# A graph-network layer on one core: the node update stored in runs of consecutive nodes, the flag for the general pass computed inside the loop, and the last three edge groups as softmax batches of their own

## The chip, the cores and the metric

The kernel runs on one core of one Trainium2 chip. The core has five engines, each with its own queue of instructions that it takes in order: TensorE (PE in the profile, with its weight loads shown apart as PEld), VectorE (DVE), ScalarE (ACT), GpSimd (POOL) and SyncE (SP). [...] Sixteen DMA engines move data between the chip's memory (HBM) and the on-chip memory (SBUF); matrix products land in PSUM. The metric is the device time of one execution in microseconds (us), and the figure that counts is the median of several executions.

## What is computed

One message-passing layer over 12,500 nodes with 64 features and 412,500 edges sorted by receiver, each with 32 features. The reference, cut to what matters:

```python
def layer(node_features, edge_features, senders, receivers, ...):
    act = jax.nn.swish
    msg_in = concatenate([node_features[senders], node_features[receivers], edge_features], -1)
    messages = act(msg_in @ W1 + b1) @ W2 + b2
    att_logits = act(msg_in @ Wa1 + ba1) @ Wa2 + ba2
    att = jax.nn.softmax(att_logits, axis=0)            # over ALL edges
    messages = messages * att
    aggregated = segment_sum(messages, receivers, num_segments=n_nodes)
    upd_in = concatenate([node_features, aggregated], -1)
    return act(upd_in @ Wu1 + bu1) @ Wu2 + bu2

h = maximum(layernorm(x), 0)
x = x + layer(h, edge_attr_32, src, dst, ...)
```

The softmax is over all the edges at once, so nothing can be normalised until the last edge has been seen; and the node update at the end needs the finished sums of all messages.

## The kernel before

**Node phase.** The nodes are padded to NP = 12,544 = 128 x NB with NB = 98; node number = p * 98 + b. The layer norm is computed and two tables of 128 columns go to HBM: `ts_d`, what a sender adds to the hidden layer, and `tr_d`, what a receiver adds.

**Edge loop** (`one_pass`, lines 278 to 555). The edges go through in NG = 403 groups of 1,024 (K = 8 columns of 128). For each group:

- `load(g)` (L351), called two groups ahead: POOL issues 8 indirect DMAs (L358) that gather the senders' rows of `ts_d` into `gs`; SP fetches the edge features, the receivers' numbers and a window of `tr_d`; DVE builds a one-hot matrix (`eo`, L379); PE adds edge and receiver part into `pe` (L385).
- `begin(g)` (L388): DVE adds `pe` to `gs` (L390), which waits for the gathers; ACT takes the tanh (L391).
- `end(g)` (L393): DVE forms the message activations (`acts`, L399), the attention activations (L402), multiplies by the attention vector (L404) and sums to logits `lg` (L407). At the end of a batch, `top` (L411) finds the maximum and PE transposes it (L422, tile `mt`).
- `weigh(s)` (L425): running maximum `nmax`, rescale factor `scale`, exponentials `p` for the batch s.
- `sum_up(g)` (L492), a generator in three steps that lags the loop by about five groups: one-hot of receivers in a window of 40 nodes (L442), weights (L452), 8 matmuls into `sp` (L456), copy (L462), projection to the 64 hidden units of the node update (L467), and `put` (L469), which adds the result into `sums` in SBUF (L477, L480) and notes the maximum in force (L481).

A batch is B = 4 groups. `starts` (L289) makes batches of four, then one of two groups (400 and 401) and one of one group (402). A group can only be summed after its batch has been weighed. After the last groups (L539 to 544) what has not yet been summed is drained: at g = 400 up to group 398, at g = 401 all the rest up to 401, before `begin(402)` comes on DVE's queue, and at g = 402 the last group. `pin` fixes the program order of an instruction within its engine's queue; what is not pinned, a list scheduler places.

During groups 16 and later, `node_bias` (L252) computes each node's own part of the update, four columns b at a time, and stores it to `bu_d`; `node_rest` stores x plus the output bias in `xb_d`.

**Node update** (L558 to 601). When `sums` is complete, 13 chunks of 8 columns b (the last one of 2) are processed, the two halves of a chunk stacked on partitions 0 to 63 and 64 to 127. `sums` holds node p * 98 + b at that very column, while a chunk wants the nodes ordered b first:

```python
sv = sums[:, :NP].rearrange("f (p b) -> f b p", b=NB)     # L563
```

so ACT (L581, `fac`) and DVE (L586, `uT`, once per half) read `sums` with a step of 98 words from element to element. Then DVE adds the bias `bu_in` (L589), ACT takes the tanh (L591), DVE finishes the swish (L592), PE does n matmuls with `uT[:, i, :]` as the weights (L596), DVE adds `xb` (L598), and SP stores the result (L601). Tiles rotate through 3 buffers (`fac` and `th` through 2). Chunk c is written below as L598(c) and so on.

**Flag.** If a receiver falls out of its window, a general pass (`general`) must redo everything. `far` holds three maxima that are known by group 40; after the node update `worst` is formed from them (L604 to 613), combined through `res` tiles so that it follows the last stores, and written to `wrong`. Every engine then loads `wrong` into a register (L246) and branches past `general` (L248).

Of the kernel before, what the change touches and what calls it, by code (L numbers as in the profile page):

```python
# [41 lines left out]
F32 = mybir.dt.float32  # L42
I32 = mybir.dt.int32
AF = mybir.ActivationFunctionType
ALU = mybir.AluOpType
AX = mybir.AxisListType
# [4 lines left out]
P = 128  # L51
D = 64
DE = 32
U = 64
C = 2 * U
# [19 lines left out]
def gnn_kernel(ctx: ExitStack, tc: tile.TileContext, n_edges, x, src, dst, dst_row, first, edge,  # L75
# [14 lines left out]
    hT_d = dram.tile([D, NB, P], F32, name="hT_d")  # L90
    bu_d = dram.tile([U, NB, P], F32, name="bu_d")
    xb_d = dram.tile([NP, D], F32, name="xb_d")

# [157 lines left out]

def node_bias(tc, b, v, work, ps):  # L252

    nc = tc.nc
    NB, w_node = v["NB"], v["w_node"]
    n = min(4, NB - b)
    hb = work.tile([D + 1, 4, P], F32, name="hb")
    nc.vector.memset(hb[D:, :, :], 1.0)
    nc.sync.dma_start(hb[:D, :n, :], v["hT_d"][:, b:b + n, :])
    pb = ps.tile([P, 4, P], F32, name="mt")  # L260
    nc.tensor.matmul(pb[:U, :n, :], w_node[:, 2 * C:], hb[:, :n, :], start=True, stop=True)
    bu = work.tile([U, 4, P], F32, name="bu")
    nc.scalar.copy(bu[:, :n, :], pb[:U, :n, :])
    nc.sync.dma_start(v["bu_d"][:, b:b + n, :], bu[:, :n, :])

# [12 lines left out]
def one_pass(tc, n_edges, v):  # L278
# [4 lines left out]
                       "far", "wrong"))  # L283
    ts_d, tr_d, bu_d, edge, dst_row = (v[k] for k in ("ts_d", "tr_d", "bu_d", "edge", "dst_row"))
    wa2, ba2_c, w2b, wu1a, wu2, we, gather = (
        v[k] for k in ("wa2", "ba2_c", "w2b", "wu1a", "wu2", "we", "gather"))
    ACTS, WINS, AHEAD = 8, 3, 2

    starts = list(range(0, NG - 1, B)) + [NG - 1]  # L289
    NS = len(starts)  # L290
# [4 lines left out]
    with ExitStack() as ctx:  # L295
# [27 lines left out]
        with tc.tile_pool(name="work2", bufs=2) as work2, \  # L323
# [64 lines left out]
            def begin(g):  # L388

                pin(nc.vector.tensor_tensor(gss[g], pes[g], gss[g], ALU.add))  # L390
                pin(nc.scalar.activation(pes[g], gss[g], AF.Tanh))  # L391

            def end(g):  # L393

                s = batch[g]
                if g == starts[s]:
                    lgs[s] = small.tile([P, B * K], F32, name="lg")
                gs, th = gss.pop(g), pes.pop(g)
                pin(nc.vector.scalar_tensor_tensor(acts[g % ACTS][:, :, 0:U], th[:, :, U:C], 1.0,  # L399
                                                   gs[:, :, U:C], op0=ALU.add, op1=ALU.mult))  # L400
                att = work2.tile([P, K, U], F32, name="att")
# [6 lines left out]
                if g == starts[s] + size[s] - 1:  # L408
                    mts[s] = top(s)

            def top(s):  # L411
# [106 lines left out]
            for g in range(NG):  # L518
                more = None
                if done <= g - B - 1 and g < NG - 1 or g == NG - 2 and done < starts[batch[g]]:  # L520
                    more, done = sum_up(done), done + 1
                begin(g)
                if more:
                    next(more)
# [13 lines left out]

                if g >= NG - 3:  # L539
                    upto = starts[batch[g]] - 1 if g == NG - 3 else g + 1  # L540
                    for i in list(range(done, upto)) + [None, None] * (g > NG - 3):
                        for _ in sum_up(i):
                            pass
                    done = max(done, upto)
                if g == min(30, NG):
# [3 lines left out]
                if g == min(40, NG):  # L549
                    pin(nc.vector.tensor_reduce(far[:, 1:2], dloc, AX.X, ALU.min, negate=True))  # L550
                if g >= 16 and g // 4 - 4 < -(-NB // 4):
                    if g % 4 == 2:
                        node_bias(tc, (g // 4 - 4) * 4, v, work2, one_ps)
                    elif g % 4 == 0:
                        node_rest(tc, (g // 4 - 4) * 4, v, work2)


        with tc.tile_pool(name="upd1", bufs=1) as upd1, \  # L558
# [3 lines left out]
            out_v = v["out"].rearrange("(p b) d -> p b d", b=NB)  # L562
            sv = sums[:, :NP].rearrange("f (p b) -> f b p", b=NB)  # L563
            last = nmax[:, NS:NS + 1]
            ones = upd1.tile([P, P], F32, name="ones")
            nc.vector.memset(ones, 1.0)
            all_ps = upd_ps.tile([P, P], F32, name="worst_ps", bufs=1)
            nc.tensor.matmul(all_ps[:, 0:1], ones, total, start=True, stop=True)
            inv = upd1.tile([P, 1], F32, name="inv")
            nc.vector.reciprocal(inv, all_ps[:, 0:1])  # L570

            assert NB % 2 == 0
            for c in range(0, NB, 2 * H):
                n = min(H, (NB - c) // 2)
                bu = work.tile([P, H, P], F32, name="bu_in")
                for h in range(2):
                    nc.sync.dma_start(bu[h * U:(h + 1) * U, :n, :], bu_d[:, c + h * n:c + (h + 1) * n, :])
                xb = work.tile([P, 2 * H, D], F32, name="xb")
                nc.sync.dma_start(xb[:, :2 * n, :], xb_v[:, c:c + 2 * n, :])
                fac = work.tile([U, 2 * H, P], F32, name="fac", bufs=2)  # L580
                nc.scalar.activation(fac[:, :2 * n, :], sv[U:, c:c + 2 * n, :], AF.Exp, bias=last[U:],  # L581
                                     scale=-1.0)
                uT = work.tile([P, H, P], F32, name="uT")
                for h in range(2):
                    cols = slice(h * n, (h + 1) * n)
                    nc.vector.scalar_tensor_tensor(  # L586
                        uT[h * U:(h + 1) * U, :n, :], sv[:U, c + h * n:c + (h + 1) * n, :], inv[:U],
                        fac[:, cols, :], op0=ALU.mult, op1=ALU.mult)
                nc.vector.tensor_tensor(uT[:, :n, :], uT[:, :n, :], bu[:, :n, :], ALU.add)  # L589
                th = work.tile([P, H, P], F32, name="th", bufs=2)  # L590
                nc.scalar.activation(th[:, :n, :], uT[:, :n, :], AF.Tanh, scale=0.5)  # L591
                nc.vector.scalar_tensor_tensor(uT[:, :n, :], th[:, :n, :], 1.0, uT[:, :n, :],  # L592
                                               op0=ALU.add, op1=ALU.mult)
                po = upd_ps.tile([P, H, 2, D], F32, name="po")
                for i in range(n):
                    nc.tensor.matmul(po[:, i, :, :], uT[:, i, :], wu2h, start=True, stop=True)  # L596
                res = work.tile([P, 2 * H, D], F32, name="res")
# [5 lines left out]

            worst = upd1.tile([P, 1], F32, name="worst")  # L604
            nc.vector.tensor_reduce(worst, far, AX.X, ALU.max)
            worst_ps = upd_ps.tile([P, P], F32, name="worst_ps", bufs=1)
            nc.tensor.transpose(worst_ps, worst.to_broadcast([P, P]), ident)
            nc.vector.tensor_reduce(worst, worst_ps, AX.X, ALU.max)
            two = [work.tile([P, 2 * H, D], F32, name="res") for _ in range(3)]
            for t in two:  # L610
                nc.vector.tensor_scalar(t[:, 0, 0:1], worst, 0.0, None, op0=ALU.is_gt)
            nc.vector.tensor_tensor(two[0][:, 0, 0:1], two[0][:, 0, 0:1], two[1][:, 0, 0:1], ALU.max)
            nc.vector.tensor_tensor(wrong, two[0][:, 0, 0:1], two[2][:, 0, 0:1], ALU.max)

# [217 lines left out]
```

## Time and profile before

| | us |
|---|---|
| median of 3 runs (lowest, highest) | 4304.88 (4300.02, 4320.17) |
| the profiled execution, its own time | 4310.41 |
| its span, first to last instruction | 4308.7 |
| POOL busy in the span, almost all of it gather issues | 3166.1 |
| DVE busy | 2544.5 |
| PE busy (modelled ends) | 2221.4 |
| ACT busy | 595.8 |

| stretch of the profiled execution | from, to (us) |
|---|---|
| last gather issue of POOL | 4220.68, 4221.62 |
| `begin(402)` on DVE (L390) | 4229.27 |
| last write to `sums` (L481) ends | 4240.82 |
| last L598 ends | 4297.13 |
| `wrong` written (L613) ends | 4298.58 |
| end of the span | 4308.7 |

A row of a group reads: line, engine, operation, output <- input with their shapes, count, then total busy time and mean ns, and the idle time in front with what ended it. In a timeline a row has start, duration, engine, line, operation, and in brackets the idle time before it and its releaser. Engine names with a q (SPq, DVEq) are an engine's instruction sequencer.

### The profile page before, as it was taken

Reading aid. Unit: us, or ns where it says so; the run is one execution under the profiler, and the core shown is the slowest. Engines: PE = TensorE matmul, PEld = TensorE weight load, DVE = VectorE, ACT = ScalarE, POOL = GpSimd, SP = SyncE. Lnnn points to the kernel's source line nnn. Section 1 sums busy time; section 2 is a strip of 40 time slices with the busy share of each in tenths; the row PEclk is TensorE's granted clock in tenths of the full one; section 3 lists DMA queues with packets and bytes.
Section 4 is the critical chain, followed back from the end, with each engine's and each line's share of the span. In section 5 each row is a group of like instructions: output and inputs, shape, how many; then the busy total and the mean of one; then the engine's idle time right before and its main releaser. Section 6 shows DMA issues by size and latency. Waiting matters only on the chain.

```text
span 4308.7 us, 41469 instructions
## 1 busy us (share of the span) xinstructions
PE 2221.4 (52%) x11224; PEld 1681.3 (39%) x11224; DVE 2544.5 (59%) x4914; ACT 595.8 (14%) x1212; POOL 3166.1 (73%) x3237
## 2 busy tenths in 40 slices
PE   6644544644445555544444555555554444545554
PEld 6533333433334434433333334444343333334443
DVE  6755655655556555556555565555565555655557
ACT  2211111111111111111111111111111111111113
POOL 2777777777777777777777777777777777777771
PEclk8657676576766555666666665555566666665555
DMA  6533334333333333333333333333333333333323
GB/s 199 144 81 96 94 96 99 92 97 93 97 93 80 86 87 78 88 88 78 87 84 81 88 80 85 87 78 88 88 78 87 84 81 88 80 86 87 78 75 101
DMA packets 227005, 391.95 MB, mean 91 GB/s; under 512 B 98890, under 2 KB 151179, under 8 KB 213707
## 3 DMA queue, kind: packets, MB, share of 16 engines
q0 software_dynamic: 103168, 211.49, 20.1%
q1 hardware_dynamic: 120580, 167.79, 15.0%
q10 hardware_dynamic: 3014, 9.92, 0.8%
q8 instruction: 93, 1.52, 0.2%
q14 instruction: 150, 1.22, 0.1%
HBM read 363.16 MB, written 25.72 MB: 90 GB/s over the span
## 4 chain that ended last, share of the span: by engine, by line
POOL 42%; issue 26%; DMA 14%; DVE 9%; PE 8%; DVEq 0%; ACT 0%; ACTq 0%; POOLq 0%; SPq 0%
POOL gs L358 42%; DMA gs<-ts_d,src_sb 13%; PE pe L385 5%; DVE eo L379 2%; PE sp L456 2%; DVE gs L390 1%; DVE att L404 1%; DVE sums L481 1%; PE mt L467 1%; DVE sums L480 1%; PE pn L228 1%; DVE uT L586 1%; DVE lg L407 0%; DVE wt L452 0%; DVE oh L442 0%
## 5 line engine op out<-in xcount | busy, mean ns | idle before, releaser
L358 POOL DMA_INDIRECT gs<-ts_d,src_sb x3224 | 3154.0, 978 | 1054.6 <-issue 900.8
L385 PE MATMUL pe<-wins,eo 128*128 128x256 f32 x3224 | 1348.6, 591 | 1248.7 <-issue 1170.2
L385 PEld LDWEIGHTS pe<-wins,eo 128*128 128x128 f32 x3224 | 926.1, 301 | 1514.2 <-issue 1216.5
L390 DVE TENSOR_TENSOR gs<-pe,gs 128x1024 f32<-128x1024 f32 x403 | 491.5, 1220 | 1398.2 <-DMA gs<-ts_d,src_sb 1394.5
L391 ACT ACTIVATE pe<-gs 128x1024 f32<-128x1024 f32 x403 | 413.4, 1026 | 2962.2 <-DVE gs L390 2661.2
L456 PE MATMUL sp<-wt,acts 128*65 128x40 f32 x6448 | 581.7, 260 | 3.0 <-DVE wt L452 3.0
L456 PEld LDWEIGHTS sp<-wt,acts 128*65 128x65 f32 x6448 | 531.1, 172 | 28.3 <-DVE wt L452 3.5
L422 PE MATMUL mt<-ident,mx 128*128 128x128 f32 x102 | 48.4, 474 | 676.2 <-DVE sums L480 668.1
L399 DVE SCALAR_TENSOR_TENSOR acts<-pe,gs 128x512 f32<-128x512 f32 x403 | 275.4, 683 | 56.7 <-ACT pe L391 56.7
L422 PEld LDWEIGHTS mt<-ident,mx 128*128 128x128 f32 x102 | 18.5, 182 | 688.8 <-DVE sums L480 679.9
L404 DVE TENSOR_TENSOR att<-att,wa 128x512 f32<-128x512 f32 x403 | 277.6, 689 | 9.7
L407 DVE TENSOR_REDUCE lg<-att 128x8 f32<-128x512 f32 x403 | 275.0, 682 | 10.3
L379 DVE TENSOR_TENSOR eo<-db,bj 64x512 f32<-64x512 int32 x403 | 275.9, 685 | 7.3
L402 DVE SCALAR_TENSOR_TENSOR att<-pe,gs 128x512 f32<-128x512 f32 x403 | 273.4, 678 | 0.0
L467 PEld LDWEIGHTS mt<-ss,w2u 65*64 65x64 f32 x806 | 97.5, 171 | 292.0 <-issue 223.2
L452 DVE TENSOR_TENSOR wt<-oh,p 128x320 f32<-128x320 f32 x403 | 197.3, 490 | 9.8
L442 DVE TENSOR_TENSOR oh<-dloc,iota_w 128x320 f32<-128x320 f32 x403 | 192.1, 477 | 0.1
L467 PE MATMUL mt<-ss,w2u 65*64 65x40 f32 x806 | 147.8, 276 | 68.2 <-ACT ss L462 42.3
L477 DVE SCALAR_TENSOR_TENSOR sums<-sums,scale,mt 64x40 f32 x102 | 25.3, 248 | 167.5 <-PE mt L467 167.5
L481 DVE COPY sums<-nmax 64x40 f32 x403 | 77.2, 192 | 9.3 <-issue 0.2
L433 ACT ACTIVATE scale<-fall 128x1 f32<-128x1 f32 x102 | 20.7, 203 | 427.0 <-DVE fall L432 427.0
L462 ACT COPY ss<-sp 65x40 f32<-65x40 f32 x403 | 73.5, 182 | 23.8 <-PE sp L456 23.2
(97 smaller groups left out, 763.6 us busy)
## 6 DMA issues: line engine op xcount, KB each, us to landing
gs<-ts_d,src_sb POOLq DMA_INDIRECT x3224
eo<-in_edge_dram SPq DMA_DIRECT2D x100, 512.0 KB
db<-in_dst_row_dram SPq DMA_DIRECT2D x200, 256.0 KB
wins<-tr_d SPq DMA_DIRECT2D x806, 32.0 KB
ts_d<-ts SPq DMA_DIRECT2D x7, 896.0 KB
tr_d<-tr ACTq DMA_DIRECT2D x7, 896.0 KB
xc<-in_x_dram SPq DMA_DIRECT2D x7, 448.0 KB
hT_d<-hT ACTq DMA_DIRECT2D x7, 448.0 KB
```

Source lines behind the costliest of these rows:

```text
L358: nc.gpsimd.indirect_dma_start(out=gs[:, j, :], out_offset=None, in_=ts_d[:, :], in_offset=bass.IndirectOffsetOnAxis(ap=src_sb[:, t + j:t ...
L379: pin(nc.vector.tensor_tensor(eo[:WR, :].rearrange("p (h e) -> p h e", h=2), db.rearrange("p (h e) -> p h e", h=2), bj[:, g, :, None].to_b ...
L385: pin(nc.tensor.matmul(pe[:, 2 * q:2 * q + 2, :], eo[:, q * P:(q + 1) * P], win[:, q // 2, :, :], start=True, stop=True))
L390: pin(nc.vector.tensor_tensor(gss[g], pes[g], gss[g], ALU.add))
L391: pin(nc.scalar.activation(pes[g], gss[g], AF.Tanh))
L399: pin(nc.vector.scalar_tensor_tensor(acts[g % ACTS][:, :, 0:U], th[:, :, U:C], 1.0, gs[:, :, U:C], op0=ALU.add, op1=ALU.mult))
L402: pin(nc.vector.scalar_tensor_tensor(att, th[:, :, 0:U], 1.0, gs[:, :, 0:U], op0=ALU.add, op1=ALU.mult))
L404: pin(nc.vector.tensor_tensor(att, att, wa2[:, None, :].to_broadcast([P, K, U]), ALU.mult))
L407: pin(nc.vector.tensor_reduce(lgs[s][:, k:k + K], att, AX.X, ALU.add))
L452: pin(nc.vector.tensor_tensor(wt, ohs.pop(g), ps_[batch[g]][:, k:k + K, None].to_broadcast([P, K, W]), ALU.mult))
L456: pin(nc.tensor.matmul(sp, acts[g % ACTS][:, j, :], wt[:, j, :], start=j == 0, stop=j == K - 1))
L467: pin(nc.tensor.matmul(pp, w2u, sps.pop(g), start=True, stop=True))
```

## The change

1. **Node order in the update.** A chunk keeps the order of `sums`: p outside, b inside. `sums` is now read in runs of 8 (ACT) or 4 (DVE) neighbouring words. `uT`, `bu_in` and `th` hold the order (p b) with b = 4 innermost, and the matmuls take their weights as `uv[:, :, i]`, every fourth word. To make the bias fit, `node_bias` writes its copy out of PSUM in that order (a step of 4 words) and stores to a second buffer `bq_d`. Numbers and sizes of the instructions and DMAs stay as they were; the last chunk has n = 1.
2. **Flag in the loop.** `worst` is reduced and transposed at group 44, reduced again and compared into `wrong` at group 45. After the node update three one-element memsets take the place of the five small instructions.
3. **Last groups.** `starts` ends in three batches of one group each (400, 401, 402), so there are 103 batches in place of 102. From g = NG - 4 on, groups are summed as soon as they are weighed; at g = 402 the step that copies `sp` is issued ahead of `begin`, and its `acts` are formed after the batch's maximum.

The diff, cut to its core:

```diff
+    bq_d = dram.tile([U, NP], F32, name="bq_d")
...
-    nc.scalar.copy(bu[:, :n, :], pb[:U, :n, :])
-    nc.sync.dma_start(v["bu_d"][:, b:b + n, :], bu[:, :n, :])
+    if quads and n == 4:
+        nc.scalar.copy(bu.rearrange("u b p -> u (b p)").rearrange("u (p b) -> u b p", b=4), pb[:U])
+    else:
+        nc.scalar.copy(bu[:, :n, :], pb[:U, :n, :])
+    to = v["bq_d"].rearrange("u (b p) -> u b p", p=P) if quads else v["bu_d"]
+    nc.sync.dma_start(to[:, b:b + n, :], bu[:, :n, :])
...
-    starts = list(range(0, NG - 1, B)) + [NG - 1]
+    starts = list(range(0, NG - 3, B)) + [NG - 3, NG - 2, NG - 1]
...
-                pin(nc.vector.scalar_tensor_tensor(acts[g % ACTS][:, :, 0:U], th[:, :, U:C], 1.0,
-                                                   gs[:, :, U:C], op0=ALU.add, op1=ALU.mult))
+                if g < NG - 1:
+                    message()
...
+                if g == NG - 1:
+                    message()
...
-                if done <= g - B - 1 and g < NG - 1 or g == NG - 2 and done < starts[batch[g]]:
+                if done <= g - B - 1 or g >= NG - 3 and done < g:
                     more, done = sum_up(done), done + 1
+                if more and g == NG - 1:
+                    next(more)
                 begin(g)
-                if more:
+                if more and g < NG - 1:
                     next(more)
...
-                if g >= NG - 3:
-                    upto = starts[batch[g]] - 1 if g == NG - 3 else g + 1
-                    for i in list(range(done, upto)) + [None, None] * (g > NG - 3):
+                if g >= NG - 4:
+                    upto = g + (-3, -1, 0, 1)[g - NG + 4]
+                    for i in list(range(done, upto)) + [None, None] * (g == NG - 1):
                         for _ in sum_up(i):
                             pass
+                        if i == done and g < NG - 1:
+                            weigh_upto(batch[g])
...
+                if g == min(44, NG):
+                    worst = small.tile([P, 1], F32, name="worst", bufs=1)
+                    pin(nc.vector.tensor_reduce(worst, far, AX.X, ALU.max))
+                    worst_ps = one_ps.tile([P, 4, P], F32, name="mt")[:, 0, :]
+                    pin(nc.tensor.transpose(worst_ps, worst.to_broadcast([P, P]), ident))
+                if g == min(45, NG):
+                    pin(nc.vector.tensor_reduce(worst, worst_ps, AX.X, ALU.max))
+                    pin(nc.vector.tensor_scalar(wrong, worst, 0.0, None, op0=ALU.is_gt))
...
-            sv = sums[:, :NP].rearrange("f (p b) -> f b p", b=NB)
+            sv = sums[:, :NP].rearrange("f (p b) -> f p b", b=NB)
...
-                fac = work.tile([U, 2 * H, P], F32, name="fac", bufs=2)
-                nc.scalar.activation(fac[:, :2 * n, :], sv[U:, c:c + 2 * n, :], AF.Exp, bias=last[U:],
-                                     scale=-1.0)
-                uT = work.tile([P, H, P], F32, name="uT")
+                fac = work.tile([U, P * 2 * H], F32, name="fac", bufs=2)[:, :P * 2 * n].rearrange(
+                    "u (p b) -> u p b", b=2 * n)
+                nc.scalar.activation(fac, sv[U:, :, c:c + 2 * n], AF.Exp, bias=last[U:], scale=-1.0)
+                uT = work.tile([P, P * H], F32, name="uT")[:, :P * n]
+                uv = uT.rearrange("u (p b) -> u p b", b=n)
                 for h in range(2):
...
                     nc.vector.scalar_tensor_tensor(
-                        uT[h * U:(h + 1) * U, :n, :], sv[:U, c + h * n:c + (h + 1) * n, :], inv[:U],
-                        fac[:, cols, :], op0=ALU.mult, op1=ALU.mult)
+                        uv[h * U:(h + 1) * U], sv[:U, :, c + h * n:c + (h + 1) * n], inv[:U],
+                        fac[:, :, h * n:(h + 1) * n], op0=ALU.mult, op1=ALU.mult)
...
-                    nc.tensor.matmul(po[:, i, :, :], uT[:, i, :], wu2h, start=True, stop=True)
+                    nc.tensor.matmul(po[:, i, :, :], uv[:, :, i], wu2h, start=True, stop=True)
...
-            worst = upd1.tile([P, 1], F32, name="worst")
-            nc.vector.tensor_reduce(worst, far, AX.X, ALU.max)
-            worst_ps = upd_ps.tile([P, P], F32, name="worst_ps", bufs=1)
-            nc.tensor.transpose(worst_ps, worst.to_broadcast([P, P]), ident)
-            nc.vector.tensor_reduce(worst, worst_ps, AX.X, ALU.max)
-            two = [work.tile([P, 2 * H, D], F32, name="res") for _ in range(3)]
...
-            nc.vector.tensor_tensor(wrong, two[0][:, 0, 0:1], two[2][:, 0, 0:1], ALU.max)
+            for _ in range(3):
+                pin(nc.vector.memset(work.tile([P, 2 * H, D], F32, name="res")[:, 0, 0:1], 0.0))
```

## The prediction, written before the changed kernel ran

> **What bounds the kernel now.** I read the page first: the slices, the chain and the costliest group.
>
> ```profile
> POOL 2777777777777777777777777777777777777771
> ...
> L358 POOL DMA_INDIRECT gs<-ts_d,src_sb x3224 | 3154.0, 978 | 1054.6 <-issue 900.8
> ```
>
> POOL is equally full from the first loop slice to the last: 3224 gather issues at 0.98 us plus about 0.3 us between them, some 4.1 ms of the 4308.7. Put against each other, the instruction orders of the two kernels have the same POOL stream, row for row. So the loop keeps its pace as long as nothing makes POOL wait, and all that can move lies behind POOL's last issue: 4308.7 - 4221.6 = 87 us, 2% of the time. There I read the timeline, then the groups by form from 4240.9 on, then the rows of the two lines that end the program.
>
> ```profile
> 4220.68 0.94 POOL L358 DMA_INDIRECT gs<-ts_d,src_sb  x1 [0.30 <-issue]
> ...
> 4228.75 0.19 DVE L480 TENSOR_TENSOR sums<-sums,mt 64x40 f32 x1 [2.21 <-PE mt L467]
> 4228.97 0.18 DVE L481 COPY sums<-nmax 64x40 f32 x1
> 4229.27 1.22 DVE L390 TENSOR_TENSOR gs<-pe,gs 128x1024 f32<-128x1024 f32 x1
> ...
> 4240.64 0.18 DVE L481 COPY sums<-nmax 64x40 f32 x1
> ```
>
> The last L390 doesn't wait for its gathers: it stands in DVE's queue behind groups 399 to 401. The node update follows:
>
> ```profile
> L586 DVE SCALAR_TENSOR_TENSOR uT<-sums,inv,fac 64x512 f32<-64x512 f32 x24 | 28.0, 1165 | 0.9 <-ACT fac L581 0.3
> L581 ACT ACTIVATE fac<-sums,nmax 64x1024 f32<-64x1024 f32 x12 | 26.8, 2242 | 11.9 <-DVE uT L586 10.8 <-DVE sums L481 1.1
> L592 DVE SCALAR_TENSOR_TENSOR uT<-th,uT 128x512 f32<-128x512 f32 x12 | 8.2, 680 | 0.1
> ```
>
> DVE hardly idles: it is the bound, and L586 alone is 28 of its 53 us. The end:
>
> ```profile
> L248 SPq EVENT_SEMAPHORE  x8: 17/17/17, 4302.1 to 4304.7; - x8
> ...
> L248 POOLq INC_SWDGE_SEM  x1: 1075/1075/1075, 4303.1 to 4303.1; - x1
> ...
> L828 POOLq DRAIN  x3: 40/107/3658, 4304.2 to 4308.4; - x3
> ```
>
> All engines load the flag at 4298.6 and branch; POOL then has its 1.08 us instruction and a drain of 3.66 us, to 4307.9, and the span ends 0.8 later.
>
> **Part A, the last groups.** DMA traffic ends at 4223.3 (the DMA view in slices of 0.3 us), so gather 402 lands there; the usual 2.5 us of the chain, counted from 4220.68, give the same. In the new order DVE has up to L390(402) what it has now up to 4221.0 (the order from L390(401) to the put is unchanged), then one-hot, total, weights, the maximum of 401: 0.5 + 0.2 + 0.5 + 0.8, about 4222.9. So L390 starts at 4223.3, 6.0 earlier. Behind it: ACT's tanh stands behind the copy of `sp`(400), which needs PE's 16 records (1.98 each set) until 4224.9, hence starts at 4225.2, 0.65 late; the put of 400 with its scale goes ahead of L404 (0.45); L399, 0.69, leaves the chain. That chain took 11.55 (4229.27 to 4240.82) and would take 12.35: ends at 4235.65, **5.2 us gained**. With a landing like the slowest in the chain (4.84) it is 3.8.
>
> **Part B, the update.** DVE issues contiguous 128x512 operations every 0.60 us (L589, L592, L598 one after the other), L586 every 1.17. Price of L586 in runs of 4 words: between 0.60 and 1.17 us. No row has such runs. [...]
>
> If DVE stayed gapless this would be 24 x 0.57 + 1.2 (the first `fac`, which nothing hides) = 14.9 us. It will not, and this is the step that decides. Today two L586 cover PE:
>
> ```profile
> 4268.23 0.68 DVE L592 SCALAR_TENSOR_TENSOR uT<-th,uT 128x512 f32<-128x512 f32 x1
> 4268.95 2.37 DVE L586 SCALAR_TENSOR_TENSOR uT<-sums,inv,fac 64x512 f32<-64x512 f32 x2
> ...
> 4269.06 2.05 PE L596 MATMUL po<-wu2h,uT 128*128 128x128 f32 x8 [1.47 <-DVE uT L592]
> ...
> 4271.24 0.67 DVE L598 TENSOR_TENSOR res<-po,xb 128x512 f32<-128x512 f32 x1
> ```
>
> From L592 to its L598 at least 0.68 + 0.12 + 2.07 + 0.13 = 3.0 us. DVE's order repeats every three chunks and is the same in both kernels: 589(3) 586 586 592(3) 589(4) 586 592(4) 589(5) 598(3) 586 598(4) 592(5) 586 586 598(5). At 0.60 each: 598(5) comes 1.8 after 592(5), so it waits 1.1 to 1.2; 598(4) comes 2.4 after 592(4): 0.6; 592(4) comes 1.2 after 589(4) and needs 0.68 + 0.63 of tanh + handovers, 1.4: 0.2. A period takes 15 x 0.60 + 1.9 = 10.9 in place of 12.6 (L598 at 4258.60, 4271.24, 4283.81). Start to 598(2): 17.8 becomes 13.2 (nine L586 give 5.1, `fac` 1.2, the waits take 1.9). Two periods: 3.4. From 598(8) to the end: 13.3 becomes 11.65. Together 4.5 + 3.4 + 1.65 = **9.6 us gained**.
>
> ACT has 1.05 + 0.63 per chunk of 3.6. DMA: 0.79 MB per chunk of 3.6 us is 216 GB/s where single slices reach 370 to 410; SP's issues come to 2.1 us per chunk. Both still hide; if a bias came 1 us late in each of four periods it would cost 4.
>
> **The weights of L596.** `uv[:, :, i]` takes every fourth word. PE's records are spaced 2.07/8 = 0.26 us (granted clock 0.50); those of L385 with twice the columns 0.47, so the spacing follows the moving side, and some 0.05 of the load shows. [...] By the row (loads hidden) PE keeps 2.07 per chunk. [...] Each us on PE is three waits a period, 12 us in all. I take 2.07, nearest to the rows; ends 2.07 and 4.1. Below 2.07 lies the clock: it was 0.86 from 4280 to 4284, after two dense chunks, and the eight records took 1.13 there.
>
> **Part C, the flag and the end.** The loop gains a reduce, a transpose and a reduce with compare: 0.16 + 0.48 + 0.29 + 0.15. In group 45 PE's projection waits for tile `mt` until DVE has read it, some 4 us; eight matmuls and the products of group 48 stand behind it. DVE waits 3 to 7 us per group for gathers, which covers this; uncovered, 5 us once. `node_bias`'s copy (0.58, 24 of them) may double on ACT, which is 14% busy: nothing; uncovered 14. At the end the reading of `far` was hidden; three memsets at 0.2 replace five operations and a wait: 598(12) to DVE's load of the flag falls from 1.5 to 0.7 to 1.3. More matters that `wrong` is known since group 45: POOL can load, branch and drain at 4222, beside the update. Then SP is last: it loads the flag 1.0 sooner, straight after its last store, and its own page of events (4298.9 to 4304.7) ends near 4303.7 on the old scale; with its drain and the final 0.8, 4305.3: **3.4 us gained**; ends 0.4 (every engine waits as now) and 4.4.
>
> **Sum.** 5.2 + 9.6 + 3.4 = 18.2 us. The profiled execution, 4310.41, becomes 4292.2; the median of the runs shown is 5.5 lower, so 4286.7, rounded to 4286.
>
> **Rivals.** *DVE stays gapless.* PE is denser, gaps shrink from 4.5 to about 3.3 us, the clock rises as at 4280, PE takes 1.13 and only small waits are left: B gives 15, in all 24, 4281. For it: that stretch of 0.86; against: 0.50 elsewhere. *Weights half shown*, 2.6 per chunk: B gives 3.4, in all 12, 4293. [...] *The end does not move*: POOL held as now, 3 less, 4289; inside the first case.
>
> **How the numbers follow.** What a measurement of this kernel can tell is about 0.5%, 21.5 us; faster begins at 4283.4. The forecast (0.50) lies near that edge: with 3 to 4 us for its terms and as much for the medians, half of it. Gapless 0.33, mostly faster; half shown 0.12, the same; slower side 0.05, of which most is within 0.5%. Faster 0.25 + 0.29 = 0.54, same 0.43, slower 0.03. Range: from the gapless case less noise, 4272, to half shown plus noise, 4300.
>
> **What would show it.** L390(402) starting at the landing near 4223; L586 near 680 ns and `fac` near 1050; L596's eight records 2.0 to 2.1 and L598 now waiting for PE; POOL's branch before the update. It is wrong if L586 stays above 900, if PE's set exceeds 2.6, if DVE waits for `bu_in`, or if the loop's last gather moves by more than 3 us.

## The result, and the profile after

| | before | after |
|---|---|---|
| median of the executions of one comparison (us) | 4315.44 (8, 4300.02 to 4320.17) | 4295.65 (8, 4279.81 to 4304.30) |
| the profiled execution, its own time | 4310.41 | 4301.24 |
| its span | 4308.7 | 4299.5 |

A comparison is a series of executions of a kernel with executions of the kernel before beside it; in brackets stand their number, the lowest and the highest. The ratio after to before is 0.9958, with a 95% interval of 0.9939 to 0.9977: 19.8 us less, and anything from 10 to 26 us by the interval. That is faster, and yet within the 0.5% that was named as what can be told from no change. A second comparison gave 4299.2 against 4315.5, ratio 0.9967 (0.9949 to 0.9985), 16.3 us.

The page of the changed kernel first (slices, then the costliest group):

```profile
POOL 1777777777777777777777777777777777777772
...
L364 POOL DMA_INDIRECT gs<-ts_d,src_sb x3224 | 3147.7, 976 | 1067.1 <-issue 886.9
```

POOL's issues are what they were, and still the bound of the loop. So the span is cut at marks that both kernels have: the first and the last gather issue, the last write to `sums`, the last result addition, the end.

| stretch (us, profiled executions) | before | after | difference |
|---|---|---|---|
| start to first gather issue (node phase) | 85.4 | 97.8 | +12.4 |
| first to end of last gather issue (loop) | 4136.2 | 4130.0 | -6.2 |
| A: to the end of the last write to `sums` | 19.2 | 14.3 | -4.9 |
| B: to the end of the last result addition | 56.3 | 49.3 | -7.0 |
| C: to the end of the span | 11.6 | 8.1 | -3.4 |
| behind the last gather issue, A + B + C | 87.1 | 71.7 | -15.4 |

The three stretches that the change touches gave 15.4 us; the profiled execution shows only 9.2 of it, since its node phase, which no line of the change touches, was 12.4 us longer. Both have to be explained.

Stretch A in the timeline of the changed kernel (start, duration, what, in brackets the idle time before it and its releaser):

```profile
4226.88 0.94 POOL L364 DMA_INDIRECT gs<-ts_d,src_sb  x1 [0.30 <-DMA gs<-ts_d,src_sb]
...
4230.53 1.23 DVE L396 TENSOR_TENSOR gs<-pe,gs 128x1024 f32<-128x1024 f32 x1 [2.96 <-DMA gs<-ts_d,src_sb]
...
4241.93 0.18 DVE L494 COPY sums<-nmax 64x40 f32 x1
```

The last L396 now waits for its gathers, where before it stood behind VectorE's own work with no wait. It starts 2.71 us after the last issue ended (before: 7.65). In the trace the last packet of POOL's queue ends 2.24 us after that issue (before: 2.26), and the addition begins 0.47 us later.

Stretch B, the groups by form from 4242 to 4292:

```profile
L612 DVE SCALAR_TENSOR_TENSOR uT<-sums,inv,fac 64x512 f32<-64x512 f32 x24 | 17.8, 743 | 0.7
L608 ACT ACTIVATE fac<-sums,nmax 64x1024 f32<-64x1024 f32 x12 | 13.7, 1146 | 12.2 <-DVE uT L612 10.5 <-DVE sums L494 1.1
L623 DVE TENSOR_TENSOR res<-po,xb 128x512 f32<-128x512 f32 x12 | 8.3, 690 | 4.7 <-PE po L621 4.7
L618 DVE SCALAR_TENSOR_TENSOR uT<-th,uT 128x512 f32<-128x512 f32 x12 | 8.2, 682 | 0.1
```

The products fell from 1165 to 743 ns and `fac` from 2242 to 1146. The result addition L623 has a wait for PE that it did not have. One instance of it, from the timeline:

```profile
4264.89 0.68 DVE L618 SCALAR_TENSOR_TENSOR uT<-th,uT 128x512 f32<-128x512 f32 x1
...
4265.61 1.52 DVE L612 SCALAR_TENSOR_TENSOR uT<-sums,inv,fac 64x512 f32<-64x512 f32 x2
...
4265.72 2.21 PE L621 MATMUL po<-wu2h,uT 128*128 128x128 f32 x8 [1.47 <-DVE uT L618]
...
4267.96 0.69 DVE L623 TENSOR_TENSOR res<-po,xb 128x512 f32<-128x512 f32 x1 [0.84 <-PE po L621]
```

Two products took 2.37 us and covered PE's eight matmuls; at 1.52 they no longer do, and 0.84 us comes back as a wait.

Stretch C, the instructions of the branch (count, shortest, median and longest ns, first and last start):

```profile
L249 SPq EVENT_SEMAPHORE  x8: 17/17/17, 4295.4 to 4297.8; - x8
...
L249 POOLq COMPARE_BRANCH  x1: 53/53/53, 4219.8 to 4219.8; - x1
L249 POOLq INC_SWDGE_SEM  x1: 1075/1075/1075, 4230.5 to 4230.5; - x1
```

POOL branches on the flag at 4219.8, beside other work, and its long instruction and its drain of 3.66 us are over at 4235.3, before the update begins. SP's page of events is now the last thing, 1.7 us before the end of the span.

### The profile page after: what moved, and what is told of

Its sections match the earlier page's. It is cut to its first block, busy times and chain, and to the rows that moved or that the text cites. A ratio compares the mean times of both kernels' runs of the same rounds, so it can differ in the third digit from the quotient of the medians.

```text
span 4299.5 us, 41478 instructions
## 1 busy us (share of the span) xinstructions
PE 2221.7 (52%) x11225; PEld 1691.8 (39%) x11225; DVE 2535.4 (59%) x4919; ACT 594.6 (14%) x1215; POOL 3159.8 (73%) x3237
## 3 DMA queue, kind: packets, MB, share of 16 engines
q0 software_dynamic: 103168, 211.49, 18.2%
q8 instruction: 93, 1.52, 0.2%
## 4 chain that ended last, share of the span: by engine, by line
## 5 line engine op out<-in xcount | busy, mean ns | idle before, releaser
L391 PE MATMUL pe<-wins,eo 128*128 128x256 f32 x3224 | 1332.2, 585 | 1234.4 <-issue 1160.3
L396 DVE TENSOR_TENSOR gs<-pe,gs 128x1024 f32<-128x1024 f32 x403 | 491.7, 1220 | 1390.7 <-DMA gs<-ts_d,src_sb 1386.8
L435 PEld LDWEIGHTS mt<-ident,mx 128*128 128x128 f32 x103 | 18.7, 181 | 688.6 <-DVE sums L493 682.8
```

Of the source, the lines that this page charges most:

```text
L391: pin(nc.tensor.matmul(pe[:, 2 * q:2 * q + 2, :], eo[:, q * P:(q + 1) * P], win[:, q // 2, :, :], start=True, stop=True))
```

## The experiments

Each kernel is read by the stretches of its profiled execution, in us. The changed kernel and its repeat stand in the same table: behind the last gather issue they agree to 0.2 us. The four kernels below them have one execution each, and only their stretches are read, not their times.

| kernel | node phase | loop | A | B | C | span |
|---|---|---|---|---|---|---|
| before | 85.4 | 4136.2 | 19.2 | 56.3 | 11.6 | 4308.7 |
| after | 97.8 | 4130.0 | 14.3 | 49.3 | 8.1 | 4299.5 |
| after, repeated | 83.7 | 4136.0 | 14.5 | 49.3 | 8.0 | 4291.5 |
| order of the nodes alone | 84.9 | 4139.2 | 18.7 | 50.0 | 11.7 | 4304.4 |
| flag in the loop alone | 98.1 | 4136.9 | 18.7 | 55.8 | 8.4 | 4317.8 |
| last groups alone | 84.0 | 4134.5 | 14.3 | 55.4 | 11.8 | 4300.1 |
| after, contiguous weights | 98.1 | 4139.4 | 14.3 | 45.5 | 7.9 | 4305.1 |

### The three parts, one at a time

The first kernel takes only the new node order (with `bq_d`), the second only the flag, the third only `starts` and the order of the last groups, each as in the diff above.

> The kernel before with part 1 alone (node order of the update). Theory: the gain of this part lies wholly between the last write to sums and the last result addition, 56.3 us before and 49.3 in the changed kernel: 49 to 50 here, with the first operation on sums near 743 ns and fac near 1146; the stretches ahead of it (last gather issue to last write to sums, 19.2) and behind it (last result to end of span, 11.6) stay within 1.2 us. Rival (the parts lean on each other, for instance the early branch of POOL or the earlier flag frees the update): this stretch stays above 52. Rival (the gain is in the loop's pace): the stretch is anything, but the time from the first gather issue to the last falls by more than 6 us against 4135.3.

> The kernel before with part 2 alone (flag in the loop). Theory: last result to end of span falls from 11.6 to about 8.1 us, because POOL branches and drains before the update and SP loads the flag without a wait; the update stays at 56 and the last groups at 19 us. Rival (POOL's drain was beside the other engines' branches and cost nothing): it falls by 1.5 us at most, from the smaller operations alone. A cost in the loop would show as POOL idle around group 45, over 0.3 us at one issue.

> The kernel before with part 3 alone (last three groups as batches of their own). Theory: last gather issue (its end) to last write to sums falls from 19.2 to about 14.3 us, 13.2 if the last gather lands after 2.5 and not 3.6 us; the last L390-like addition waits for its gather and no more for DVE's queue. Rival (the work only moves, PE or ACT is late in its place): not under 17 us.

Each part acts in its own stretch. The order takes 6.3 us from B and leaves C at 11.7; the flag takes 3.2 from C; the last groups take 4.9 from A. The flag costs nothing in the loop that these traces show: from the first gather issue of group 40 to that of group 56 POOL takes 166.3 us with it and 166.9 before. The three shortenings behind the last issue, 6.8, 4.2 and 5.6, make 16.6 against 15.4 for all together: nearly additive. Of the excess 1.0 us comes from A, which is 0.5 shorter in each of the two kernels that don't touch it. The last L390 shows what part 3 does. In the kernel with the order alone, then in that with the last groups alone:

```profile
4223.18 0.94 POOL L364 DMA_INDIRECT gs<-ts_d,src_sb  x1 [0.30 <-issue]
4231.24 1.23 DVE L396 TENSOR_TENSOR gs<-pe,gs 128x1024 f32<-128x1024 f32 x1
```

```profile
4217.65 0.94 POOL L358 DMA_INDIRECT gs<-ts_d,src_sb  x1 [0.30 <-issue]
4221.31 1.23 DVE L390 TENSOR_TENSOR gs<-pe,gs 128x1024 f32<-128x1024 f32 x1 [2.96 <-DMA gs<-ts_d,src_sb]
```

Issue to addition is 8.1 us without a wait in the one, 3.7 us with a wait of 2.96 for the DMA in the other.

### Contiguous weights

```diff
-                    nc.tensor.matmul(po[:, i, :, :], uv[:, :, i], wu2h, ...)
+                    nc.tensor.matmul(po[:, i, :, :], uT[:, i * P:(i + 1) * P], wu2h, ...)
```

In this kernel the output holds its nodes in another order; the work is the same.

> The changed kernel, but the update's matmuls take contiguous weights (columns i*128 to i*128+127 in place of every fourth word): the rows of the output come in another order, all instructions keep their number and size. Theory (a strided weight load of 128 words takes about 0.26 us whatever the granted clock, and is then PE's limit): eight records take 2.05 to 2.1 us at clock 0.5 and 1.1 to 1.3 where the clock is over 0.8, and from the last write to sums to the last result it takes 0.5 to 4 us less than 49.3. Rival (the load is hidden, PE's spacing follows the moving side): eight records stay at 2.1 to 2.2 as in the changed kernel and the stretch stays within 0.5 us of it.

B fell by 3.8 us, to 45.5. The groups from 4248 on:

```profile
L621 PE MATMUL po<-wu2h,uT 128*128 128x128 f32 x98 | 21.7, 389 | 22.6 <-DVE uT L618 22.4
...
L623 DVE TENSOR_TENSOR res<-po,xb 128x512 f32<-128x512 f32 x12 | 8.2, 685 | 1.1 <-PE po L621 1.0
```

The wait of L623 shrank from 4.7 to 1.0. Why, is seen when eight records are put beside the granted clock. L621 alone in two windows, first of this kernel, then of the changed one (window, its length, PE busy, PEld busy, granted clock, DMA share, GB/s):

```profile
4274.80:4276.00 1.20, 1.13 (x8) 0.95 (x8) 1.00 0.88 306
```

```profile
4277.30:4279.50 2.20, 2.11 (x8) 1.94 (x8) 0.96 0.90 291
```

At nearly the same clock eight matmuls take 1.13 us with contiguous weights and 2.11 with every fourth word, 0.14 and 0.26 each. At a clock of 0.50 they take 2.04 to 2.08 and 2.20 to 2.24. So the strided load shows with 0.16 us a set at 0.50, and with 0.98 at the faster clock.

So the 3.8 us hang on the clock of this one execution. It was 1.00 for 10.6 us of B here, and for 8.7 and 6.8 us in the two of the changed kernel, where eight matmuls with strided loads still took 2.11 us at 0.96. At 0.50 throughout, nine waits shorter by 0.16 us would give some 1.4 us, an estimate from these rows that no run tested.

### The layout of `fac`

```diff
-                    "u (p b) -> u p b", b=2 * n)
+                    "u (h p b) -> u p h b", h=2, b=n)
...
-                        fac[:, :, h * n:(h + 1) * n], op0=ALU.mult, op1=ALU.mult)
+                        fac[:, :, h, :], op0=ALU.mult, op1=ALU.mult)
```

This kernel, the first pipelined one and the first with idle transposes, below, ran on another chip, on which the kernel before took 5493.21 us (51 executions). The stretches behind the loop have the same lengths there (B of this kernel 49.3), so they are compared; the loop is not.

> The changed kernel with fac laid out half by half, so that the product at L612 reads fac in one contiguous run and sums in runs of four words as before; ScalarE writes the same 1024 words. Theory one (every stream with runs of four words adds to the price): L612 falls from a pitch of 0.755 us to about 0.68 us, and the last stretch by about a microsecond at most. Theory two (the runs of four in sums alone set the price): L612 stays at 0.75 us and nothing moves. Third: the price comes from fac alone, L612 falls to 0.60 us. If ScalarE's write is what costs its 1.146 us, fac changes too; I expect it between 1.03 and 1.15 us.

```profile
L612 DVE SCALAR_TENSOR_TENSOR uT<-sums,inv,fac 64x512 f32<-64x512 f32 x24 | 17.8, 743 | 0.7
L608 ACT ACTIVATE fac<-sums,nmax 64x1024 f32<-64x1024 f32 x12 | 13.7, 1146 | 12.2 <-DVE uT L612 10.5 <-DVE sums L494 1.1
```

Both rows are unchanged to the nanosecond. How `fac` is laid out costs nothing here; the excess of L612 over 0.60 us lies elsewhere, most likely in the reading of `sums` in runs of four. That is not shown: this run varied neither `sums` nor the one-column factor `inv`.

### Pipelining the update

If L623 waits because too little stands between L618 and it, a whole chunk can be put between. In each step of the pinned order: `fac` and the products of chunk k, L618 and the matmuls of k-1, bias and tanh of k, the result of k-2.

```diff
+            for k in range(NC + 2):
+                if k < NC:
+                    begin_chunk(k)          # fac, then the two products
+                if 1 <= k <= NC:
+                    swish_chunk(k - 1)      # L618, eight matmuls
+                if k < NC:
+                    bias_chunk(k)           # L615, tanh
+                if k >= 2:
+                    end_chunk(k - 2)        # L623, store
```

> The changed kernel with its update pipelined by a pinned order: in each step VectorE runs the two products (L612) of chunk k, then the swish product of chunk k-1 (and with it the eight matmuls of k-1), the bias addition of k, and the result addition of k-2. Theory: in the changed kernel a period of three chunks takes 11.5 us where VectorE's own work is 3 x (2 x 0.755 + 3 x 0.60) = 9.9 us, and the rest is the wait of the result addition for the strided-weight matmuls (2.1 to 2.2 us a chunk). With one whole chunk of VectorE's work (3.3 us) between swish and result that wait goes: three chunks in 9.9 to 10.2 us, last write to sums to last result addition 43 to 45 us instead of 49.3, time 4 to 6 us below the changed kernel's. Rival: the input DMAs on SP's queue, or ScalarE (1.15 + 0.6 us a chunk) with its round trip through tanh, end last instead: that stretch stays at 47 us or more.

A miss, by the way that the rival named: B became 62.0 us, 12.7 longer, and the ratio to before was 1.0003 (0.9989 to 1.0016). One step of its timeline:

```profile
5430.79 0.63 ACT L626 ACTIVATE th<-uT 128x512 f32<-128x512 f32 x1 [2.95 <-DVE uT L624]
...
5431.44 1.15 ACT L613 ACTIVATE fac<-sums,nmax 64x1024 f32<-64x1024 f32 x1
...
5432.62 0.74 DVE L617 SCALAR_TENSOR_TENSOR uT<-sums,inv,fac 64x512 f32<-64x512 f32 x1 [1.33 <-ACT fac L613]
```

The wait for PE is gone, but there is a ring: the products wait for `fac`, `fac` stands in ScalarE's queue behind a tanh, and that tanh waits for the bias addition, which stands behind the products of its own chunk. Once round takes 4.75 us. ScalarE is busy for some 22 of the 62 us; its order was wrong. The next kernel makes `fac` one chunk ahead:

```diff
+            fac_chunk(0)
             for k in range(NC + 2):
+                if k + 1 < NC:
+                    fac_chunk(k + 1)
                 if k < NC:
-                    begin_chunk(k)          # fac, then the two products
+                    begin_chunk(k)          # the two products
```

> The pipelined update once more, but ScalarE makes fac one chunk ahead of the products. In the first pipelined version a chunk took 4.75 us, because ScalarE's order was tanh of chunk k, then fac of k+1 (1.15 us), and the products of k+1 waited 1.3 to 1.9 us for that fac, while fac waited for a tanh that itself waited for the products. Theory: that ring was all; with fac made ahead no engine waits, a chunk takes VectorE's own 3.3 us, last write to sums to last result addition 42 to 45 us instead of 49.3 in the changed kernel, 4 to 7 us less time in all. Rival: the order of the input loads on SP's queue (five DMA issues a chunk, about 2.6 us) or ScalarE's 1.8 us a chunk with its latency ends last: that stretch at 47 us or more.

```profile
4259.19 0.69 DVE L632 TENSOR_TENSOR uT<-uT,bu_in 128x512 f32<-128x512 f32 x1
...
4259.42 2.20 PE L642 MATMUL po<-wu2h,uT 128*128 128x128 f32 x8 [1.13 <-DVE uT L639]
4259.79 0.69 DVE L648 TENSOR_TENSOR res<-po,xb 128x512 f32<-128x512 f32 x1
...
4260.39 1.50 DVE L625 SCALAR_TENSOR_TENSOR uT<-sums,inv,fac 64x512 f32<-64x512 f32 x2
```

No VectorE row has a bracket: VectorE goes from one to the next without a pause, 3.34 us a chunk. B is 44.5 us, 4.8 less than in the changed kernel, with the strided weights still in and the clock at 0.50 through the whole update. The median was 4291.53 (7 executions) against 4299.2 for the changed kernel in the same comparison, the ratio to before 0.9950 (0.9933 to 0.9968). The two kernels' intervals overlap; it is the stretch that shows the gain.

### What sets the node phase

The first three late node phases (97.8, 98.1, 98.1) were those of the three kernels that set the flag in the loop. So the flag was the first suspect. The two executions of one and the same changed kernel clear it, as do the two pipelined kernels (85.2 and 85.0), which set the flag in the loop too; the weight loads of PE in the node phase, first after (late), then its repeat (early):

```profile
47.50 0.61 PEld L225 LDWEIGHTS pt<-ident,h 128*64 128x64 f32 x4 [0.38 <-DVE hT L226]
48.15 3.54 PEld L229 LDWEIGHTS pn<-w_node,hT 65*128 65x128 f32 x16
```

```profile
47.43 0.36 PEld L225 LDWEIGHTS pt<-ident,h 128*64 128x64 f32 x4 [0.38 <-DVE hT L226]
47.79 1.87 PEld L229 LDWEIGHTS pn<-w_node,hT 65*128 65x128 f32 x16
```

In the expectations from here on, "gate" is the author's word for the switch of the granted clock between 0.50 and 1.00: open is 1.00, closed is 0.50.

> The changed kernel again, unaltered. Its three parts took 15.4 us off the stretch behind the last gather issue in the first profile (87.1 to 71.7 us), while its node phase was 12.4 us longer. If the clock gate sets the node phase by chance, the first gather issue may stand anywhere from 85 to 98 us, weight loads before it taking 0.11 to 0.12 us where it is early and 0.21 to 0.23 us where it is late, and the mean over runs is 10 to 20 us below before. If the flag in the loop makes the node phase late: 97 to 98 us again.

The same sixteen loads take 0.22 us each in one execution and 0.117 in the other. Over all of 50 to 60 us PE is then busy 10.0 or 8.2 us of ten:

```profile
50.00:60.00 10.00, 9.99 (x47) 8.96 (x46) 5.64 (x10) 4.52 (x8) 0.00 (x0) 1.00 0.43 121
```

```profile
50.00:60.00 10.00, 8.22 (x66) 7.26 (x67) 8.97 (x15) 4.98 (x10) 0.00 (x0) 1.00 0.58 161
```

(Columns: PE, PEld, DVE, ACT, POOL busy with their instructions, then the granted clock.) The clock is given as 1.00 in both. The clock changes that the traces recorded explain that: the first, to 1.00, stands at 47.39 us in the repeat and at 87.74 in the first execution, and ahead of its first record the column shows 1.00 for want of one. From there on clock and loads agree. The first record stands where the loads drop to the fast pitch: at 37.33 us (order alone), 47.39 to 50.37 (before, last groups alone, the other `fac` layout, the repeat, the two pipelined kernels) or 87.74 to 88.33 (the three late ones). The kernel with the order alone falls back from 61.2 to 74.9 us, and the column shows it:

```profile
61.50:74.00 12.50, 12.05 (x55) 10.10 (x53) 5.72 (x10) 2.35 (x5) 0.00 (x0) 0.50 0.62 185
```

The kernel with the other `fac` layout falls back from 65.1 to 78.8 us, and its node phase lies in between, at 88.6.

What raises the clock, and why at another moment in each execution, these runs don't show. PE's busy time alone does not: in the late execution PE was busy for 11.15 of the 11.6 us from 37.4 to 49, and nearly without a gap to 87, before the first record of 1.00 at 87.74, and the fence above has the clock at 0.50 for 12.5 us while PE was busy for 12.05.

The author guessed that work on PE raises it all the same. Then idle work on PE should bring the rise forward, here transposes whose result is read by nobody:

```diff
+        def busy(m):
+            for _ in range(m):
+                tc.keep_in_program_order(nc.tensor.transpose(idle, zero[:, :D], ident))
+
+        busy(40)
         for c in range(0, NB, CB):
...
                 nc.scalar.copy(ts[:, b:b + n, :], pn[:, :n, :])
+                if c < 3 * CB:
+                    busy(8)
```

It was put into the changed kernel, into the first pipelined one, into the one with `fac` ahead, and, with `c + b < 24` in place of `c < 3 * CB`, once more into that.

> The changed kernel with idle transposes on TensorE in the node phase: 40 before the first real one and 8 after each of the first twelve groups of four blocks; their result is read by nobody. Question: the first gather issue stands at 84 to 85 us in three profiles and at 98 us in three, and the three late ones are the three kernels that set the flag in the loop. [...] With the idle transposes TensorE has no gap, the gate opens by about 30 us, loads take 0.11 to 0.12 us, and the first gather issue stands at 83 to 87 us though the flag is still set in the loop: 11 to 13 us below the profiled execution of the changed kernel. Theory two (the flag in the loop delays the node phase by itself): the first gather issue stays at 97 to 98 us, or later by the added work.

> The pipelined update and the idle transposes together, on the changed kernel. If both theories hold, their gains add: first gather issue at 83 to 87 us, last write to sums to last result addition 43 to 45 us, and 4277 to 4285 us in all, that is 15 to 18 us below the profiled changed kernel. If the gate is not what delays the node phase: no better than the pipelined update alone.

> The same pipelined update with fac ahead, and the idle transposes on TensorE in the node phase. If both theories hold: first gather issue at 84 to 89 us in the profile, the update in 42 to 45 us, and 4 to 18 us below the changed kernel beside it, according to where its own node phase falls; 20 to 30 us below before. If the update stays at 47 us or more: no more than the idle transposes bring.

> The pipelined update with fac ahead, and idle transposes on TensorE only where they were seen to act: 40 before the first real transpose and 8 after each of the first seven groups of four blocks, in place of twelve. In the kernel with all of them weight loads went from 0.21 us to 0.11 us at about 32 us and stayed there, but the first gather issue stood at 88.7 us, 4 to 5 us later than where the gate opened early by itself, because some 64 idle transposes still ran after that. Theory: the first gather issue stands at 85 to 87 us, the runs lie within 6 us of each other, and the median is 1 to 4 us below that kernel's, about 4288 to 4291 us on a chip where before takes 4315 us. Rival: without the later ones the gate closes again in the node phase; then loads return to 0.21 us before 80 us, the first gather issue stands at 90 us or later in the profile, and the runs spread as the changed kernel's do.

| idle transposes in | node phase | B | comparison's median, lowest to highest (us) | ratio to before |
|---|---|---|---|---|
| after (other chip) | 88.3 | 49.3 | 5480.12, 5468.80 to 5496.93 | 0.9976 (0.9964 to 0.9989) |
| pipelined (other chip) | 87.8 | 62.8 | 5489.12, 5475.91 to 5513.12 | 0.9991 (0.9976 to 1.0007) |
| pipelined, `fac` ahead | 88.7 | 46.2 | 4291.91, 4290.09 to 4294.73 | 0.9945 (0.9928 to 0.9962) |
| the same, fewer of them | 82.9 | 44.7 | 4290.20, 4286.16 to 4294.69 | 0.9938 (0.9922 to 0.9954) |

The loads of the last of these from 29 us on:

```profile
29.49 1.22 PEld L236 LDWEIGHTS pn<-w_node,hT 65*128 65x128 f32 x8
30.63 0.88 PEld L205 LDWEIGHTS idle<-ident,zero 128*64 128x64 f32 x8
```

With the 40 transposes ahead the clock goes to 1.00 at 4 to 8 us, in all four kernels, but back to 0.50 6.8 us later, before the real matmuls begin at 23 us. Once the eight per group have begun, at 28 us, it goes to 1.00 at 30 to 33 us and stays there to 78 to 86 us. In the last kernel, whose idle work ends at 45 us, it falls at 77.8 us. The rival had named 80 us for that, but also a first gather issue at 90 us or later, and it stands at 82.9; in kernels without idle work the clock falls at about that time as well (before at 81.1, the repeat at 81.5).

No node phase of the four is late. The first two landed some 1 us past the 87 us that were expected, from the idle transposes that still ran after the clock had risen; the last came 2 us ahead of its 85. On the chips with the usual loop the executions lie closer, within 4.6 and 8.5 us (6 executions each; 6 us were expected of the last), where those of the changed kernel in two comparisons spread over 24.5 and 22.3 and those with `fac` ahead and no idle work over 18.1 (9 and 8, and 7 executions). The median did not fall: 4291.91 with the idle work against 4291.53 without, in one comparison. The last kernel has the lowest median, 4290.20, but in another comparison and with an interval that overlaps theirs.

The update missed what was expected in two of the four: the pipelined kernel still has the ring (62.8 for 43 to 45), and with `fac` ahead B is 46.2 for 42 to 45, since the first bias load came late and VectorE waited 1.76 us for it.

## Why the prediction was right, and where it was not

**The size of the gain.** 18.2 us were forecast; the two comparisons gave 19.8 and 16.3, the stretches of the profile 15.4. That the first comes within 2 us is luck, since its interval spans 16 us; the stretches are the better measure, and they fall 2.8 short, nearly all of it in part B. The forecast of 4286 lies 9.7 us below the measured 4295.65, inside its range, mostly since it started from the 4304.88 of three executions, while eight of the same kernel have 4315.44. A gain beyond 0.5%, to which 0.54 was given, did not come: it was 0.42% and 0.33%. The spread between executions, some 20 us, is as large as the gain; part of it is the node phase, which the prediction took to be fixed.

**Part A**, 5.2 forecast, 4.9 measured, and that closeness is luck too, from two errors that cancel. L390(402) was to start 6.0 us earlier and starts 4.9 earlier: the prediction read the end of the DMA traffic, 1.7 us after POOL's issue, from slices of 0.3 us and took it for the landing. A last packet ended only 2.26 us after the issue, in before as well, and the addition waits some 0.5 us more. The chain behind it was to grow from 11.55 to 12.35 us and stayed at 11.6; the terms named for it (0.65 and 0.45 more, 0.69 less) make 11.96 and not 12.35. That L390 waits for its gathers and for nothing else was right.

**Part B**, 9.6 forecast, 7.0 measured. This is the step that was mis-sized. The structure held: VectorE's order is the same, it doesn't become gapless, and L598 (now L623) waits for PE. The three stretches of the sum: start to 598(2) 14.2 us against 13.2 forecast (its own terms make 13.4), two periods 23.1 against 21.8, the rest 11.9 against 11.65. Two terms were too small.

One is the price of L586 in runs of four words. It was taken at 0.60 us, the pitch of contiguous operations, which no run shows for such a product: two of them take 1.52, and one follows another after 0.75 to 0.78. The ends named were 0.60 and 1.17. The other is PE's set, taken at 2.07 and measured at 2.20 to 2.24 at the same clock of 0.50.

Redone from the rows, a period is 0.65 us longer than the 10.9 forecast (11.55). Two waits for a set that is 0.14 longer give 0.28 of that. The rest, about 0.35, is VectorE's own: 0.9 us for its six products and 0.35 because an operation ahead of a product is followed after 0.71 and not 0.60, less some 0.9 of waits that this fills. `fac` was taken at 1.05, which no run shows for runs of eight, and is 1.15, which the chain pays once.

**The weights of L596**, costed at nothing. "The spacing follows the moving side" held only while the clock was 0.50, and even there some 0.16 us a set showed. At a clock of 0.96 the strided records take 0.26 us each (2.11 / 8), where contiguous ones take 0.14 at 1.00 (1.13 / 8). The upper end of 4.1 us for a set, named in the prediction, is an estimate that no run shows: the sets took 2.11 to 2.24.

**Part C**, 3.4 forecast, 3.4 measured, by the way described: POOL's branch and drain beside other work, then SP's page of events as the last thing. The flag alone gave 3.2.

**The rivals.** *DVE stays gapless* did not occur, and its mechanism, a clock that rises with a denser update, is not borne out. The clock was 1.00 for 3.4 us of the update before and for 8.7 and 6.8 us in the two executions of the changed kernel, yet for none of it where a pipelined order made VectorE gapless (B 44.5), though PE was busy for 62% of that update and for 55% of the changed kernel's. Where it did rise, to 0.96 for a set, PE stayed at 0.26 us a record. *Weights half shown* is nearest in kind: a cost of the load, smaller than its 2.6 a chunk. The slower side, to which 0.05 was given, did not occur: PE takes 2.2 us of a chunk's 3.85. *The end does not move* fell: it moved by 3.4.

## What to carry to other kernels

Here the layout was paid by each engine that read it: the products, shorter by 0.42 us each (1165 to 743 ns), uncovered 4.7 us of waits for PE, and the strided weight load added 0.16 us a set at a clock of 0.50 and 0.98 at 0.96 to 1.00. When an engine's time shrinks, look at what its length had been covering, and reorder so that something else covers it; then follow every queue round, since one instruction at the wrong place in an idle engine's queue can make a ring (4.75 us a chunk against 3.34). And before a change worth 0.4% is judged, cut the span at common marks: a stretch that the change doesn't touch can move by nearly as much by chance (here 14.2 us).

## What had not been expected of the hardware

- The clock of TensorE rose for the node phase at 37 to 88 us into the kernel, in executions with the same instructions up to there, and with idle transposes at 30 to 33. That moved the first gather issue from 83 to 98 us; some of it can come back in the loop (between the two executions of the changed kernel 14.2 us in the node phase, 8.0 in the span). The clock column shows this only from the first recorded change on.
- PE busy for 62% of an update of 44.5 us, in even bursts, left the clock at 0.50 throughout; at 55%, in uneven ones, it rose to 1.00 twice and three times. Whether the evenness is the reason was not tested.
- Eight matmuls whose weights are every fourth word take 2.11 us at a clock of 0.96 and 2.20 to 2.24 at 0.50; with contiguous weights 1.13 at 1.00 and 2.04 to 2.08 at 0.50.
- A product that reads runs of four words from `sums` is issued every 0.75 to 0.78 us for 512 elements, contiguous operations of that size every 0.60, and one with single words every 1.17. ScalarE's `fac` has 1.15 us for 1024 elements in runs of eight, 2.24 in single words.
- On the other chip the loop took 5259.5 us (the kernel with the other `fac` layout) where it took 4130 to 4141 elsewhere, though a gather issue takes as long as elsewhere (0.94 us, the next 0.30 later). Much of the time is in waits whose releaser the profile can't place, or for which it shows none. Of that kernel from 2000 to 2400 us (who waited <- for whom: us in all, times, longest us):

```profile
ACT ss L475 <- remote: 209.4, 18, 24.9
POOL gs L364 <- issue: 160.8, 238, 11.8
```

The changed kernel's own trace of that window has no wait for a remote releaser, and none of POOL's issues there comes more than 0.3 us after the one before has ended. The kernel before was as slow on that chip (5493.21 us), so it isn't the change; what it is was not settled.
